# The order of work in the first block of an RWKV and Hadamard-FFN layer, and its last output rows in two banks

## The chip, the cores and the metric

The kernel runs on one core of a Trainium2 chip. Its engines are TensorE (PE, the matmuls), VectorE (DVE), ScalarE (ACT), GpSimd (POOL) and SyncE (SP), which here only issues DMAs. [...] The metric is the device time of one execution in microseconds; the number that counts is the median of several runs.

## What is computed

The input `x` has 4 sequences of 2048 tokens with 512 channels, in fp32. The layer is

```python
xn  = layernorm(x)                          # over the channels, no scale or shift
s   = xn shifted by one token               # zero before the first token of a sequence
r   = (mu_r*xn + (1-mu_r)*s) @ Wr.T         # the same for k and v
wkv = wkv_v4(k, v, w, u)                    # a recurrence over the tokens
att = (sigmoid(r) * wkv) @ Wo.T
h   = silu(xn @ W1.T) * (xn @ W3.T)         # 2048 hidden features
ffn = fwht(h) @ W2.T                        # Walsh-Hadamard transform over the 2048
out = x + att + ffn
```

## The kernel before

**Blocks.** The 8192 tokens are worked on in 8 blocks of `TB` = 1024 tokens. Tokens lie along the free dimension, channels on the 128 partitions: `xnT` holds a block of normalized activations as `NB` = 4 channel blocks of 128. A block has a projection stage (r, k, v), an up stage of 16 groups (one for each 128 features of W1 and W3), and a down stage of seven products (W2 with the Hadamard transform folded in, and Wo). From the second block on the projections, and in all blocks up and down, a 2x2 block product is made with seven products in place of eight, so that weights are brought into seven "forms". The recurrence (`wkv`) is cut into pieces that are handed out to DVE and ACT during the up stage by `step()`.

**Order.** All five engines are wrapped in `InOrder` (lines 24 to 36), which keeps each instruction in program order on its engine. So the order of the source is the order of each queue, and every row of the profile shows line 34, that of the wrapper. Groups of instructions are told apart by the names of their tiles: `bank` is PSUM, `tf` holds the mixed input of k (later, forms of the tokens), `hid` the hidden features, `part` the weight forms of an up group, `df` scratch for down forms, `dw` the down weights.

**PSUM.** There are eight banks of 128x512, given out in rotation by `bank()` (lines 89 to 91). A matmul into a bank waits until its last content has been read.

**The first block** (lines 553 to 615) can't be prepared during a block before it. The tokens come in two halves of 512 (`half`), and for each half:

- `first_statistics` (159): mean and variance of each token on DVE, and the power -0.5 on POOL.
- `first_spread` (162): per 128 tokens, a diagonal of the scale (made by DVE) and one of the shift (made by ACT), and two matmuls with a matrix of ones that spread scale and shift over all partitions into two banks.
- `first_normalized` (173): for each of four channel blocks, DVE multiplies and adds from these banks, and then `mixed_block` (180) mixes the block with its shifted self for k: ACT writes `(1-mu)*before` to `tf`, DVE adds `mu*here`.
- `projected` (196): four matmuls, one for each channel block, into one bank, and a copy by ACT to `k_sb`, `v_sb` or (with tanh) `r_sb`. There are four such groups for each half.

In between PE folds the Hadamard matrix into W2: `fold_products(n, m)` (419) multiplies rows n to m of `fold` (an alias of the upper half of `hid`), two matmuls for each row, and ACT evicts each at once with a scale. The eight rows are folded in four portions: rows 0 and 1 ahead of the first spread, 2 and 3 after it, 4 and 5 after the normalization of the second half, 6 and 7 in the second projection (v). The butterflies over these rows (`fold_butterflies`, 427) then run on DVE, and the third projection (r) follows.

**The up stage of the first block** (643 to 650) also makes the down weights. For group j below `NR` = 10, `down_forms(j)` (447) makes the forms on POOL from folded rows, or, for the last two, from Wo, which it loads first into a `df` tile; it stores them to `down_w`. Then `load_parts` for group j+2 loads a `part` and POOL makes its four forms. Both tile kinds come from rings: `ring_a` has three slots, `ring_b` two. SP issues all of these DMAs in this order, POOL makes all forms in this order.

**The down stage** (`down`, 475): seven products, each for two groups of 128 output rows, each of 10 matmuls of 512 columns. The last product's results are added to the residual by DVE (`c21`, 546) and stored by SP.

Of the kernel before, what the change touches and what calls it, by code (L numbers as in the profile page):

```python
# [8 lines left out]
F32 = mybir.dt.float32  # L9
AF = mybir.ActivationFunctionType  # L10
ALU = mybir.AluOpType
# [3 lines left out]
P = 128  # L15
H = 512
TB = 2 * H
TP = TB // P
OFF = 4
# [20 lines left out]
def tile_rwkv_attn_hadamard_ffn(  # L40
# [15 lines left out]
    NT, C = x.shape  # L56
    F = 2 * w2.shape[1] * P
    NB = C // P
    KH = NB // 2
    NF = F // P  # L60
    NR = (NF + NB) // 2
# [7 lines left out]
    ring_b = ctx.enter_context(tc.tile_pool(name="ring_b", bufs=2))  # L69
# [19 lines left out]
    def bank():  # L89
        turn[0] += 1  # L90
        return banks[(turn[0] - 1) % 8]
# [67 lines left out]
    def first_statistics(half):  # L159
        return token_statistics(f"f{half}", x_tok[:, half * HT : (half + 1) * HT, :])  # L160

    def first_spread(half, rs):
        diag = v_sb[:, half, :].rearrange("p (s t q) -> p s t q", s=2, q=P)
        for t in range(HT):
            dve.tensor_scalar(diag[:, 0, t], eye_sb, rs[:, 0, t : t + 1], None, ALU.mult)
            act.activation(diag[:, 1, t], eye_sb, AF.Copy, scale=rs[:, 1, t : t + 1])
        pts = []
        for s in range(2):
            pts.append(bank())
            pe.matmul(pts[s], lhsT=ones, rhs=diag[:, s].rearrange("p t q -> p (t q)"), start=True, stop=True)  # L170
        return pts

    def first_normalized(half, pts):
        for b in range(NB):
            xb = xnT[:, b, OFF + half * H : OFF + (half + 1) * H]
            dve.tensor_tensor(xb, xb, pts[0], ALU.mult)
            dve.tensor_tensor(xb, xb, pts[1], ALU.add)
            mixed_block(1, b, half * H, H)

    def mixed_block(kind, b, t0=0, n=TB):  # L180
        m = mix_of[kind][:, b, t0 : t0 + n]
        here, before = (xnT[:, b, OFF - d + t0 : OFF - d + t0 + n] for d in (0, 1))
        act.activation(m, before, AF.Copy, scale=omm[:, kind, b : b + 1])
        dve.scalar_tensor_tensor(m, here, vec[:, kind, b : b + 1], m, ALU.mult, ALU.add)

    def mixed(kind):
        for b in range(NB):
# [229 lines left out]
            sp.dma_start(out=fold[a].rearrange("p (k c) -> p k c", c=C), in_=w2[:, a])  # L417

    def fold_products(n, m):
        for a in range(n, m):  # L420
            for k in range(2):
                part = fold[a][:, ts(k, C)]
                pt = bank()
                pe.matmul(pt, lhsT=had_sb, rhs=part, start=True, stop=True)
                act.mul(part, pt, 0.5 / float(F) ** 0.5)

    def fold_butterflies():

# [15 lines left out]
            at[a], spare = spare, at[a]  # L444
        return sorted(enumerate(at), key=lambda p: p[1] is not e1)

    def down_forms(j, at):
        n, a = at[j] if j < NP else (j, None)
        t = ring_b.tile([P, 7, KH, P], F32, tag="b", name=f"df_{n}")
        far = down_w[:, :, n].rearrange("f p k c -> p f k c")  # L450
        if n < NP:
            a = a.rearrange("p (k m g c) -> p k m g c", k=2, m=2, c=P)
            seven_forms([t[:, f] for f in range(4)], a[:, 0, 0], a[:, 1, 0], a[:, 1, 1], a[:, 0, 1])
            sp.dma_start(out=far[:, 0], in_=a[:, 0, 0])
            sp.dma_start(out=far[:, 1:3], in_=a[:, 1])
            sp.dma_start(out=far[:, 3:7], in_=t[:, 0:4])
        else:
            sp.dma_start(out=t[:, 0:4], in_=wo[n - NP])
            forms_in(t)
            sp.dma_start(out=far, in_=t)  # L460

# [10 lines left out]

    order = (0, 1, 4, 6, 5, 3, 2)

    def down(i, w, between, w_after):
        y11, y12, y21, y22 = rows(0, 0), rows(0, 1), rows(1, 0), rows(1, 1)
        def product(k, pts, right, start, then):
            if k == 6:
                w_after()
            elif k:  # L480
                w.append(load_down(i, order[k + 1]))
            if k:
                next(between)
            for g in range(KH):
                for n in range(NR):
                    pe.matmul(
                        pts[g], lhsT=w[k][:, n, g, :], rhs=right[n // 2][:, n % 2, :],
                        start=start and n == 0, stop=n == NR - 1, skip_group_check=True,
                    )
                then(g)  # L490

        def difference(out, x0, x1):
            for o, p0, p1 in zip(out, x0, x1):
                dve.tensor_tensor(o, p0, p1, ALU.subtract)

        def at(mh, g, half):
            return ts(mh * KH + g, P), ds(i * TB + half * H, H)

        def residual(slot, mh, g, half):
            c, t = at(mh, g, half)  # L500
            sp.dma_start(out=slot, in_=xT[c, t])

        def store(slot, mh, g, half):
            c, t = at(mh, g, half)
            sp.dma_start(out=outT[c, t], in_=slot)

        add = dve.tensor_tensor
        pa, pb, pc = ([bank() for _ in range(KH)] for _ in range(3))
        s5 = [small.tile([P, H], F32, tag="s5", name=f"s5_{i}_d{g}") for g in range(KH)]
        for g in range(KH):  # L510
            residual(stage[g], 0, g, 0)
        product(0, pa, y11, True, lambda g: act.copy(pb[g], pa[g]))
        difference(y11, y12, y11)

        def c11(g):
            add(stage[g], pa[g], stage[g], ALU.add)
            store(stage[g], 0, g, 0)
            residual(stage[2 + g], 0, g, 1)
            residual(x22_of[g], 1, g, 1)

        product(1, pa, y21, False, c11)
        product(2, pc, y11, True, lambda g: act.copy(s5[g], pc[g]))
        difference(y12, y22, y12)
        for g in range(KH):
            add(x22_of[g], x22_of[g], s5[g], ALU.add)
        product(3, pc, y22, False, lambda g: None)
        difference(y22, y22, y11)

        def u2(g):
            act.copy(u2_of[g], pb[g])  # L530

        product(4, pb, y22, False, u2)
        difference(y21, y21, y22)
        for g in range(KH):
            add(u2_of[g], u2_of[g], stage[2 + g], ALU.add)
            add(stage[2 + g], pc[g], u2_of[g], ALU.add)
            store(stage[2 + g], 0, g, 1)
            residual(stage[g], 1, g, 0)

        def c22(g):  # L540
            add(x22_of[g], pb[g], x22_of[g], ALU.add)
            store(x22_of[g], 1, g, 1)

        product(5, pb, y12, False, c22)

        def c21(g):
            add(stage[g], pb[g], stage[g], ALU.add)
            store(stage[g], 1, g, 0)

        product(6, pb, y21, False, c21)  # L550


# [12 lines left out]
    load_channels(0, H, H)  # L565
    fold_load(4, NP)
    act.activation(weff, vec[:, 3, :], AF.Exp)
    fold_products(0, 2)
    spread_0 = first_spread(0, first_statistics(0))
    dve.tensor_scalar(omm, vec[:, 0:3, :], -1.0, 1.0, ALU.mult, ALU.add)  # L570
    dve.tensor_scalar(weff, weff, -1.0, None, ALU.mult)
    token_before(0)
    fold_products(2, 4)
    first_normalized(0, spread_0)
    first_rs = first_statistics(1)

    pending = {}
    for i in range(n_blocks):
# [13 lines left out]
        if i == 0:  # L592
            for kind, after in ((1, 2), (2, 0), (0, None)):
                w = w_next
                if after is not None:
                    w_next = load_square(i, after)
                    if kind != 1:
                        mixed(after)
                if kind == 2:
                    token_forms()  # L600
                for n in range(2 * NB):
                    if kind == 1:
                        if n == NB - 1:
                            spread_1 = first_spread(1, first_rs)
                        if n == NB:
                            first_normalized(1, spread_1)
                            fold_products(4, 6)
                            mixed(2)
                        projected(kind, w, n % NB, n // NB)
                    else:  # L610
                        projected(kind, w, n // 2, n % 2)
                    if kind == 2 and n == 2:
                        fold_products(6, NP)
                        folded = fold_butterflies()
            parts = [load_parts(i, 3 * KH + n) for n in range(2)]
        else:
# [25 lines left out]
        w_down = []  # L642
        for j in range(NF):
            if i == 0 and j < NR:
                down_forms(j, folded)
            if j + 2 < NF:
                parts.append(load_parts(i, 3 * KH + j + 2))
            if j >= NF - 2:
                w_down.append(load_down(i, order[j - NF + 2]))
            tail = up(i, j, parts.pop(0), tail, step)  # L650
# [29 lines left out]

        if not last:
            load_tokens(i + 1)
        down(i, w_down, (None for _ in range(6)) if last else next_tokens(), next_parts)


# [51 lines left out]
```

## Time and profile before

| | |
|---|---|
| timed runs, us | 3138.24, 3138.80, 3147.55; median 3138.8 |
| profiled execution, us | 3151.47 |
| its span, us | 3149.7 |
| PE busy | 3120.0 us, 99% |
| DVE busy | 2197.9 us, 70% |
| ACT busy | 874.1 us, 28% |
| POOL busy | 330.4 us, 10% |
| DMA | 334.44 MB, mean 106 GB/s |
| granted PE clock over the span | 0.995 |

The span is that of the profile, from its first to its last event; the execution's own time is 1.8 us longer. Times inside the span are counted from its start. By stage of the profiled execution:

| from to, us | what | PE busy, us | granted clock |
|---|---|---|---|
| 0 to 8.84 | loads, first statistics | 0 | 1.00 |
| 8.84 to 23.80 | folds, first spread | 11.89 | 1.00 |
| 43.16 to 60.39 | second spread, normalization | 12.12 | 0.96 |
| 74.26 to 132.62 | projections v and r | 58.36 | 1.00 |
| 132.62 to 241.94 | first block, up groups 0 to 8 | 108.32 | 1.00 |
| 241.94 to 273.57 | up groups 9 and 10 | 27.05 | 0.89 |
| 273.57 to 333.79 | up groups 11 to 15 | 60.22 | 1.00 |
| 333.79 to 3150 | first down stage, blocks 1 to 7 | 2812.06 | 1.00 |

A row of PE busy time is a sum over instructions whose ends are modelled; a fp32 matmul of the program is two MATMUL instructions. PE busy says that PE had work, not that it ran at its full clock.

### The profile page before, as it was taken

What the parts mean: (1) busy time and instruction counts of PE and PEld (TensorE: products, weight loads), DVE (VectorE), ACT (ScalarE), POOL (GpSimd) and SP (SyncE); (2) the same over time, 40 slices, a digit from 0 to 9 for tenths busy, and PEclk for the clock granted to TensorE, in tenths of its full rate; (3) what the DMA queues carried; (4) which work ended last, traced back from release to release, by engine and by line L of the source; (5) the groups of instructions that cost most, each with busy time, mean ns of one, the idle gap of its engine ahead of it and who ended that gap; (6) DMA issues with size and microseconds to landing.
All of it is one profiled execution on the core that took longest, in us unless ns stands there. A gap on an engine that the chain in (4) does not pass through costs nothing.

```text
span 3149.7 us, 20228 instructions
## 1 busy us (share of the span) xinstructions
PE 3120.0 (99%) x7232; PEld 1377.4 (44%) x7232; DVE 2197.9 (70%) x2316; ACT 874.1 (28%) x1374; POOL 330.4 (10%) x203
## 2 busy tenths in 40 slices
PE   7999999999999999999999999999999999999999
PEld 2443444444444444444444444444444444444444
DVE  4888856886478864787647876579655886658852
ACT  3232213331233302333023320333213332133310
POOL 1454112001000011000110001100011000110000
PEclk8999999999999999999999999999999999999999
DMA  4246433233322332222332224222332223322222
GB/s 149 79 150 228 144 110 107 82 125 110 117 72 82 114 127 102 82 72 112 134 107 82 71 102 159 93 72 80 132 123 99 71 82 146 123 75 80 76 100 77
DMA packets 75668, 334.44 MB, mean 106 GB/s; under 512 B 9136, under 2 KB 18352, under 8 KB 66224
## 3 DMA queue, kind: packets, MB, share of 16 engines
q1 hardware_dynamic: 75568, 333.15, 30.2%
q8 instruction: 57, 0.93, 0.1%
q14 instruction: 43, 0.35, 0.0%
HBM read 286.93 MB, written 46.19 MB: 106 GB/s over the span
## 4 chain that ended last, share of the span: by engine, by line
PE 98%; DMA 1%; DVE 1%; ACT 0%; issue 0%; SPq 0%; ACTq 0%
PE bank L34 98%; DMA part<-wpart 0%; DVE xnT L34 0%; DVE tf L34 0%; ACT tf L34 0%; DMA hid<-w 0%; ACT v_sb L34 0%; SPq L34 0%; DVE sa L34 0%; DVE bank L34 0%; DVE v_sb L34 0%; ACT k_sb L34 0%; ACT hid L34 0%; ACTq L34 0%
## 5 line engine op out<-in xcount | busy, mean ns | idle before, releaser
L34 PE MATMUL bank<-tf,part 128*128 128x512 f32 x2272 | 1043.0, 592 | 0.0
L34 PE MATMUL bank<-hid,dw 128*128 128x512 f32 x1792 | 787.3, 592 | 0.0
L34 PE MATMUL bank<-xnT,part 128*128 128x512 f32 x1536 | 723.8, 593 | 5.6 <-DMA part<-wpart 5.3
L34 PEld LDWEIGHTS bank<-tf,part 128*128 128x128 f32 x2272 | 432.0, 190 | 544.6 <-issue 515.7
L34 ACT COPY bank<-bank 128x512 f32<-128x512 f32 x526 | 299.8, 570 | 1258.7 <-PE bank L34 1257.5
L34 PEld LDWEIGHTS bank<-hid,dw 128*128 128x128 f32 x1792 | 340.5, 190 | 428.6 <-issue 426.7
L34 PEld LDWEIGHTS bank<-xnT,part 128*128 128x128 f32 x1536 | 292.1, 190 | 374.5 <-issue 364.5
L34 DVE SCALAR_TENSOR_TENSOR hid<-hid,bank 128x512 f32<-128x512 f32 x256 | 173.9, 679 | 175.0 <-ACT hid L34 174.8
L34 DVE TENSOR_TENSOR hid<-hid 128x1024 f32<-128x1024 f32 (+1 forms) x173 | 219.7, 1298 | 106.7 <-PE bank L34 105.8
L34 PE MATMUL bank<-hid,part 128*128 128x512 f32 x616 | 271.2, 592 | 0.0
L34 DVE RECIPROCAL e1b<-e1b 128x512 f32<-128x512 f32 x64 | 214.1, 3347 | 1.1
L34 PE MATMUL bank<-r_sb,dw 128*128 128x512 f32 x448 | 210.5, 592 | 0.0
L34 DVE TENSOR_TENSOR bank<-bank,s 128x512 f32<-128x512 f32 x256 | 168.2, 690 | 37.8 <-ACT bank L34 26.6
L34 ACT ACTIVATE hid<-bank 128x512 f32<-128x512 f32 x272 | 162.9, 600 | 101.9 <-PE bank L34 85.1
L34 DVE TENSOR_TENSOR hid<-hid,bank 128x512 f32<-128x512 f32 x256 | 173.5, 678 | 11.6 <-PE bank L34 7.1
L34 PEld LDWEIGHTS bank<-hid,part 128*128 128x128 f32 x616 | 117.0, 190 | 147.3 <-issue 145.4
L34 POOL TENSOR_TENSOR rs<-rs,neg_half 128x8 f32<-128x8 f32 x7 | 11.5, 1649 | 1581.6 <-DVE rs L34 1581.6
L34 DVE SCALAR_TENSOR_TENSOR hid<-xnT,vec,hid 128x1024 f32<-128x1024 f32 x64 | 93.0, 1487 | 99.9 <-ACT hid L34 99.9
L34 PEld LDWEIGHTS bank<-r_sb,dw 128*128 128x128 f32 x448 | 85.1, 190 | 107.1 <-issue 106.9
L34 ACT COPY s<-bank 128x512 f32<-128x512 f32 x128 | 75.0, 586 | 146.6 <-PE bank L34 146.6
L34 DVE TENSOR_TENSOR v_sb<-bank,v_sb 128x512 f32<-128x512 f32 x32 | 21.9, 688 | 130.2 <-PE bank L34 130.2
L34 POOL TENSOR_TENSOR tf<-xnT 128x1024 f32<-128x1024 f32 x16 | 46.5, 2904 | 599.3 <-PE bank L34 599.3
(103 smaller groups left out, 2238.9 us busy)
## 6 DMA issues: line engine op xcount, KB each, us to landing
part<-part_w SPq DMA_DIRECT2D x148, 896.0 KB, 4.6
dw<-down_w SPq DMA_DIRECT2D x56, 1280.0 KB, 6.4
part_w<-part SPq DMA_DIRECT2D x22, 896.0 KB, 6.9
k_sb<-x SPq DMA_DIRECT2D x7, 2048.0 KB, 8.3
xnT<-xT SPq DMA_DIRECT2D x7, 2048.0 KB, 9.4
v_sb<-xT SPq DMA_DIRECT2D x48, 256.0 KB, 4.4
out<-v_sb SPq DMA_DIRECT2D x48, 256.0 KB, 2.0
part<-wpart SPq DMA_DIRECT2D x22, 512.0 KB, 5.0
```

Of the source, the lines that this page charges most:

```text
L34: return self.tc.keep_in_program_order(issue(*args, **kwargs))
```

## The change

There are five edits.

1. `first_spread` is cut in two. `first_diagonals` makes the diagonals, and is called directly after the statistics; `first_spread` holds only the two matmuls. In the first half the second diagonal's four ACT instructions now come before any eviction of the fold.
2. `first_normalized` mixes one block behind the normalization: for block b DVE multiplies and adds, ACT writes the first term of block b (`mix_before`), and then DVE mixes block b-1 (`mix_here`). `mixed_block` calls both and is used as before elsewhere.
3. `fold_products` only issues matmuls and returns the list of what is to be evicted; `fold_evict` does that. The eight rows are folded as 0 ahead of the first spread, 1 and 2 behind it, 3 and 4 at the second half, 5 to 7 in the second projection. The evictions of the first two portions come behind the first half's normalization on ACT, those of the third behind the second half's.
4. `down_parts` allocates the `df` tile, and for the last two groups issues the load of Wo into it. It is called one group ahead of `down_forms`.
5. In the last block's down stage the last group of the last product is worked in two halves of 256 columns: the first in its own bank, the second in one more bank, to which ACT copies that half's partial sums. Each half is added and stored by itself. The extra bank is taken from the rotation in every block.

```diff
-    def first_spread(half, rs):
+    def first_diagonals(half, rs):
         diag = v_sb[:, half, :].rearrange("p (s t q) -> p s t q", s=2, q=P)
         for t in range(HT):
             dve.tensor_scalar(diag[:, 0, t], eye_sb, rs[:, 0, t : t + 1], None, ALU.mult)
             act.activation(diag[:, 1, t], eye_sb, AF.Copy, scale=rs[:, 1, t : t + 1])
+        return diag
+
+    def first_spread(diag):
         pts = []
...
     def first_normalized(half, pts):
-        for b in range(NB):
-            xb = xnT[:, b, OFF + half * H : OFF + (half + 1) * H]
-            dve.tensor_tensor(xb, xb, pts[0], ALU.mult)
-            dve.tensor_tensor(xb, xb, pts[1], ALU.add)
-            mixed_block(1, b, half * H, H)
...
+        for b in range(NB + 1):
+            if b < NB:
+                xb = xnT[:, b, OFF + half * H : OFF + (half + 1) * H]
+                dve.tensor_tensor(xb, xb, pts[0], ALU.mult)
+                dve.tensor_tensor(xb, xb, pts[1], ALU.add)
+                mix_before(1, b, half * H, H)
+            if b:
+                mix_here(1, b - 1, half * H, H)
+
+    def mix_before(kind, b, t0=0, n=TB):
+        m, before = mix_of[kind][:, b, t0 : t0 + n], xnT[:, b, OFF - 1 + t0 : OFF - 1 + t0 + n]
         act.activation(m, before, AF.Copy, scale=omm[:, kind, b : b + 1])
+
+    def mix_here(kind, b, t0=0, n=TB):
+        m, here = mix_of[kind][:, b, t0 : t0 + n], xnT[:, b, OFF + t0 : OFF + t0 + n]
         dve.scalar_tensor_tensor(m, here, vec[:, kind, b : b + 1], m, ALU.mult, ALU.add)
...
     def fold_products(n, m):
-        for a in range(n, m):
-            for k in range(2):
-                part = fold[a][:, ts(k, C)]
-                pt = bank()
-                pe.matmul(pt, lhsT=had_sb, rhs=part, start=True, stop=True)
-                act.mul(part, pt, 0.5 / float(F) ** 0.5)
+
+        left = []
+        for part in (fold[a][:, ts(k, C)] for a in range(n, m) for k in range(2)):
+            pt = bank()
+            pe.matmul(pt, lhsT=had_sb, rhs=part, start=True, stop=True)
+            left.append((part, pt))
+        return left
+
+    def fold_evict(left):
+        for part, pt in left:
+            act.mul(part, pt, 0.5 / float(F) ** 0.5)
...
-    def down_forms(j, at):
+    def down_parts(n):
+        t = ring_b.tile([P, 7, KH, P], F32, tag="b", name=f"df_{n}")
+        if n >= NP:
+            sp.dma_start(out=t[:, 0:4], in_=wo[n - NP])
+        return t
+
+    def down_forms(j, at, t):
         n, a = at[j] if j < NP else (j, None)
-        t = ring_b.tile([P, 7, KH, P], F32, tag="b", name=f"df_{n}")
...
-            sp.dma_start(out=t[:, 0:4], in_=wo[n - NP])
...
             for g in range(KH):
-                for n in range(NR):
-                    pe.matmul(
-                        pts[g], lhsT=w[k][:, n, g, :], rhs=right[n // 2][:, n % 2, :],
-                        start=start and n == 0, stop=n == NR - 1, skip_group_check=True,
-                    )
-                then(g)
+                whole = slice(0, H)
+                for pt, cols in ending if last and k == 6 and g == KH - 1 else [(pts[g], whole)]:
+                    for n in range(NR):
+                        pe.matmul(
+                            pt[:, cols], lhsT=w[k][:, n, g, :], rhs=right[n // 2][:, n % 2, cols],
+                            start=start and n == 0, stop=n == NR - 1, skip_group_check=True,
+                        )
+                    then(g) if cols == whole else c21(g, pt, cols)
...
+        ending = [(pb[KH - 1], slice(0, H // 2)), (bank(), slice(H // 2, H))]
...
+            if last and g == KH - 1:
+                act.copy(ending[1][0][:, H // 2 :], pb[g][:, H // 2 :])
...
-        def c21(g):
-            add(stage[g], pb[g], stage[g], ALU.add)
-            store(stage[g], 1, g, 0)
+        def c21(g, pt=None, cols=slice(0, H)):
+            add(stage[g][:, cols], (pb[g] if pt is None else pt)[:, cols], stage[g][:, cols], ALU.add)
+            c, t = at(1, g, 0)
+            sp.dma_start(out=outT[c, t][:, cols], in_=stage[g][:, cols])
...
-    fold_products(0, 2)
-    spread_0 = first_spread(0, first_statistics(0))
+    diag_0 = first_diagonals(0, first_statistics(0))
     dve.tensor_scalar(omm, vec[:, 0:3, :], -1.0, 1.0, ALU.mult, ALU.add)
     dve.tensor_scalar(weff, weff, -1.0, None, ALU.mult)
     token_before(0)
-    fold_products(2, 4)
+    left = fold_products(0, 1)
+    spread_0 = first_spread(diag_0)
+    left += fold_products(1, 3)
     first_normalized(0, spread_0)
-    first_rs = first_statistics(1)
+    fold_evict(left)
+    diag_1 = first_diagonals(1, first_statistics(1))
...
                         if n == NB - 1:
-                            spread_1 = first_spread(1, first_rs)
+                            spread_1 = first_spread(diag_1)
                         if n == NB:
+                            left = fold_products(3, 5)
                             first_normalized(1, spread_1)
-                            fold_products(4, 6)
+                            fold_evict(left)
                             mixed(2)
...
                     if kind == 2 and n == 2:
-                        fold_products(6, NP)
+                        fold_evict(fold_products(5, NP))
                         folded = fold_butterflies()
...
             if i == 0 and j < NR:
-                down_forms(j, folded)
+                t = down_parts(0) if j == 0 else t_next
+                t_next = down_parts(j + 1) if j + 1 < NR else None
+                down_forms(j, folded, t)
```

More of the change, by code (lines that the diff above doesn't have):

```diff
@@ L173, in first_normalized, with mixed_block @@
     def first_normalized(half, pts):
-        for b in range(NB):
-            xb = xnT[:, b, OFF + half * H : OFF + (half + 1) * H]
-            dve.tensor_tensor(xb, xb, pts[0], ALU.mult)
-            dve.tensor_tensor(xb, xb, pts[1], ALU.add)
-            mixed_block(1, b, half * H, H)
-    def mixed_block(kind, b, t0=0, n=TB):
-        m = mix_of[kind][:, b, t0 : t0 + n]
-        here, before = (xnT[:, b, OFF - d + t0 : OFF - d + t0 + n] for d in (0, 1))
+        for b in range(NB + 1):
[8 more added lines that the diff above has]
+        m, before = mix_of[kind][:, b, t0 : t0 + n], xnT[:, b, OFF - 1 + t0 : OFF - 1 + t0 + n]
         act.activation(m, before, AF.Copy, scale=omm[:, kind, b : b + 1])
+    def mix_here(kind, b, t0=0, n=TB):
+        m, here = mix_of[kind][:, b, t0 : t0 + n], xnT[:, b, OFF + t0 : OFF + t0 + n]
         dve.scalar_tensor_tensor(m, here, vec[:, kind, b : b + 1], m, ALU.mult, ALU.add)
+    def mixed_block(kind, b):
+        mix_before(kind, b)
+        mix_here(kind, b)
     def mixed(kind):
@@ L473, in tile_rwkv_attn_hadamard_ffn, with down @@
     order = (0, 1, 4, 6, 5, 3, 2)
-    def down(i, w, between, w_after):
+    def down(i, w, between, w_after, last):
         y11, y12, y21, y22 = rows(0, 0), rows(0, 1), rows(1, 0), rows(1, 1)
@@ L682, in tile_rwkv_attn_hadamard_ffn @@
             load_tokens(i + 1)
-        down(i, w_down, (None for _ in range(6)) if last else next_tokens(), next_parts)
+        down(i, w_down, (None for _ in range(6)) if last else next_tokens(), next_parts, last)
 def kernel(**inputs):
```

## The prediction

> **What bounds the kernel now.** I read the page's list of groups first, then the matmul engine's timeline over the first 70 us, then the chain of waits in order of time, then the busy time by windows. All program lines show as L34, the line of the ordering helper, so groups are told apart by tile names.
>
> The chain of waits (start, length, what) says where TensorE (PE) is not the bound:
>
> ```profile
> 22.24 0.72 ACT tf L34
> 22.99 0.75 DVE tf L34
> 23.74 0.61 DVE xnT L34
> 24.35 0.02 issue
> 24.37 0.70 DVE xnT L34
> 25.07 0.02 issue
> 25.09 0.73 ACT tf L34
> ...
> 60.39 175.48 PE bank L34 x403
> 235.87 5.93 DMA part<-wpart
> ...
> 252.28 6.11 DMA part<-wpart
> ...
> 273.57 2872.30 PE bank L34 x6692
> ```
>
> From 273.57 on, 6692 matmul rows take 2872.30 us, or 0.4292 us a row, with no wait. One matmul of the program (fp32, 512 columns) is two rows. The whole program has 7232 rows: at 0.4292 they need 3104.0 us. The first starts at 8.84 and the last ends at 3145.85 (3143.97 + 1.88), so 3145.85 - 8.84 - 3104.0 = 33.0 us are lost. Of these 24.2 lie before 74.26, the first matmul of the second projection (96 rows, 41.2 us of work, in 65.4 us), and 8.9 in the first block's up stage (132.62 to 333.79: 201.2 us for 448 rows, 192.3). Nothing else is to be had but the tail of 3.9 us behind the last matmul.
>
> PE's timeline shows the first half of the start (start, length, engine, operation, rows; idle time in brackets):
>
> ```profile
> 15.14 1.02 PE L34 MATMUL bank<-v_sb,ones 128*128 128x512 f32 x2
> 17.15 1.12 PE L34 MATMUL bank<-v_sb,ones 128*128 128x512 f32 x2 [0.99 <-ACT v_sb L34]
> 23.80 1.21 PE L34 MATMUL bank<-tf,w 128*128 128x512 f32 x2 [2.08 <-DVE tf L34]
> 26.65 2.07 PE L34 MATMUL bank<-tf,w 128*128 128x512 f32 x2 [1.65 <-DVE tf L34]
> 32.37 10.95 PE L34 MATMUL bank<-tf,w 128*128 128x512 f32 x18 [0.78 <-DVE tf L34]
> ```
>
> Each normalized block costs 2.86 us (23.80 to 26.65), because VectorE (DVE) waits for ScalarE's (ACT's) first mixing term and only then goes to the next block. And PE, starved, runs slow: 18 rows take 10.79 us from 32.37 to 43.16, where 7.73 would do. The granted clock (third figure from the end of a line of the windows view) says the same:
>
> ```profile
> 23.80:43.16 19.36, 16.14 (x24) 5.90 (x25) 9.85 (x25) 3.34 (x5) 1.01 (x1) 0.65 0.32 128
> 60.39:74.26 13.87, 13.87 (x27) 5.99 (x27) 4.87 (x4) 6.90 (x10) 2.33 (x1) 0.81 0.01 1
> ```
>
> The second half repeats the pattern, and its last block comes at 60.39.
>
> **The start, first half.** The first eight rows run cold: 8.84 to 15.14, so 0.857 us a row for most. Before, they are the fold of rows 0 and 1; after, four fold rows and the four spread rows. ACT's diagonals no longer stand behind four evictions (they began at 15.84): the statistics end at 9.58, four of 0.39 us end near 10.9, before PE asks at 12.3. So the first spread ends at 8.84 + 6 x 0.857 = 14.0 and the second at 15.14. DVE starts 0.2 later, as it did (16.0 to 16.20): multiply at 14.2, first add at 15.35 instead of 18.32. The channels are there: issue at 4.14, landing 8.5 us later, 12.6. DVE then runs without ACT in its loop, 0.61 + 0.70 + 0.75 = 2.06 a block: first add done 16.05, three blocks to 22.2, the last mix to 22.95, against 32.32 before.
>
> PE cannot use all of it. The banks go round by eight: two for the fold, two for the spread, four for the next fold, so the first projection gets bank 0, which is not evicted until ACT is through its four mixing terms (the last add ends 21.45, ACT's term 22.2, eviction 22.85). PE's fold ends at 18.6 (8 rows after 15.14), and it idles 4.3 us to 22.9. **Here a rule speaks against the change.** The row: the idle of 4.34 us ahead of 258.53 was followed by 12 rows in 7.76 us (258.53 to 266.29), 2.6 over the 5.15 they need; the stretch at 32.37 lost 3.06. The Trainium skill ("TensorE: Matmul & The Clock Gate", Part 1) puts the clock at half after an idle window of about 3.4 us, and back after 3.4 us of work, in a free-running window; by that the loss would be half of 3.4, 1.7 us, and a hole of 4.3 need not always hold a whole idle window. The trace is harsher: at 26.65 it is slow after two holes of 2.08 and 1.65 with work between. I take 2.8, bounds 0 and 3.1.
>
> So the projection's first three groups, 24 rows, run from 22.9 for 10.3 + 2.8 to 36.0; before, this point was 43.16. The second statistics (5.0 us on DVE) start at 22.95 and are hidden, as are ACT's second diagonals, done by 29.
>
> **The start, second half.** Spread 36.0 to 37.7, fourth group to 41.15, and two more folds, 8 rows, to 44.6. ACT's queue decides: the first mixing term stands behind the copy of the fourth group, as it does now (copy 3.64 us after the group's start, term 0.48 later). Copy at 41.35, term 41.83 to 42.55, first mix 42.6 to 43.35, then two blocks of 2.06: 45.4 and 47.45, last mix 48.3. PE takes the first block at 44.6, the second at 45.45, waits 1.2 for the third, and has the last at 48.36. The row at 241.94 (idle 1.00, then 4 rows in 1.95) says that such a hole does not slow it, so the 2.7 lost after 60.39 (26 rows in 13.87, 11.16 needed) goes too. The remaining 26 rows end at 59.5, against 74.26: 14.8 less. One fold (4 rows, 1.7 us) is moved behind this point, into the gap after the third group of the second projection. **Sum of the start: -13.0 us.** If ACT or DVE takes 10% longer in those loops, about 2 us go; without the cold stretch it is -15.8.
>
> Behind this PE is dense to the up stage, so the gain is kept. The moved fold adds two evictions ahead of the butterflies; DVE needs that part 5 us into the first pass, and is behind its own mixing until then. Cost 0; uncovered, 1.7.
>
> **Wo's parts.** The stall of the up stage is a loop: SyncE's queue (SP) issues the next part only behind the store of the down forms; GpSimd (POOL) makes these only after the forms of the part before.
>
> ```profile
> 238.26 0.42 SPq L34 DMA_DIRECT2D df<-wo  x1
> 241.93 5.03 POOL L34 TENSOR_TENSOR part<-part 128x256 f32<-128x256 f32 x4 [6.56 <-PE bank L34]
> 246.91 4.87 POOL L34 TENSOR_TENSOR df<-df 128x256 f32<-128x256 f32 x4
> 251.81 0.37 SPq L34 DMA_DIRECT2D down_w<-df  x1
> ```
>
> Wo was issued at 238.26 and landed about 7.3 later, 245.6; POOL reaches it at 246.91 with no idle, busy with the part. Loading it a group earlier moves nothing on this path. The load now sits on SP ahead of the seventh group's stores and waits there for the slot of the sixth (stored 218.65, landing 3.3 later, 222): behind it are stores and the form store of 235.4, 13 us later, so no cost. What may be won is traffic: the part issued at 252.28 no longer shares with Wo at 254.08, 6.1 against the median 5.3 us. I take -0.2, bounds -0.8 and +0.5; the stall itself stays.
>
> **The last rows.** The last group's 20 rows become 40 of 256 columns. No row of the trace has 256 columns. If the weight load (0.19 us busy) stays beside a row of 0.215, it costs nothing; if each of the 20 added loads stood bare, 3.8 us. The skill's page of TensorE ("Back-to-back issue gap") gives 262 cycles for 256 columns and 518 for 512, which over two passes and 40 rows is an estimate of 0.1 us; I take that, because 0.19 is under 0.215. DVE's last add shrinks from 0.69 to about 0.42 (by 512 columns and the 0.28 of a 128-column operation), and the store is halved: stores of 256 and 128 KB landed in 2.1 and 1.7. Sum 0.1 - 0.27 - 0.4 = -0.6, bounds -0.7 and +3.1. ACT's half copy lies in an idle ACT, over 4 us before its use. The extra bank per block turns the rotation by one in seven transitions: the fifth bank of the next stage is then the last one of the down stage, read by DVE at 454.16 to 454.85 and wanted 20 rows, 8.6 us, after 453.96. Slack 7.7; cost 0.
>
> **Sum** against the profiled run (3151.47 us, span 3149.7): -13.0 - 0.2 - 0.6 = -13.8. The timed runs are 3138.24, 3138.80 and 3147.55: the last lies 8.75 above the median, about the 8.9 of the up stage's stalls, so I read the median as a run without them and leave the Wo term out: 3138.8 - 13.6 = **3125.2**.
>
> **Rivals.** (1) Likeliest, 0.66: as above, 3121 to 3129; the no-cold case, 3122.4, is in it. (2) The start is cheaper without the profiler: profiled minus median is 12.7, the stalls explain 8.9, the other 3.8 may be start that timed runs don't lose. Then the gain is 13.6 - 3.8 = 9.8: 3129.0. For it: the median's loss over the floor is only some 20; against: the waits are sums of instruction times. 0.16. (3) The up stage stalls in the median run: 3125.2 + 8.9 = 3134.1. For it: the loop's part issues at 203.04, 219.14, 235.87 are 16 us apart where PE needs 12.0; against: one timed run of three. 0.14. (4) Slower: that loop falls behind sooner. Each further group late costs 4.3 (16.3 - 12.0) and a cold 2.6; two such groups cancel the gain, and over three more make 3138.8 - 13.6 + 8.9 + 3 x 6.9 = 3154.8. It decides if the butterflies end later relative to the up stage than now. Against: they start behind mixing that moves with the second projection (-14.8), so 1.7 earlier relative to it. 0.04. That the Wo change doesn't do what it says is part of all four.
>
> About 0.3%, 9.4 us, is what a measurement can tell from no change: faster is below 3129.4. Case 1 is wholly there, case 2 in two of three, case 3 is within: faster 0.77, same 0.19, slower 0.04. The range 3119.5 to 3134.5 takes in the missing cold stretch and case 3.
>
> **What would show it.** Right: the first spread ahead of the second fold; a hole near 4 us ahead of the first projection with DVE long ahead; second projection at 59 to 60; block 0's up stage still short of a part near the ninth and tenth group; DVE's last add near 0.42. Wrong: a hole ahead of each projection block as now, a wait behind 273 in a later block, or rows over 0.22 us in the last group.

## The result and the profile after

| | before | after |
|---|---|---|
| timed runs, us | 18: 3137.37 to 3153.59, median 3138.9 | 18: 3124.75 to 3137.65, median 3127.69 |
| profiled execution, us | 3151.47 | 3126.89 |
| its span, us | 3149.7 | 3125.1 |
| first matmul | 8.84 | 8.86 |
| second projection begins | 74.26 | 57.34 |
| PE waits for a part in the up stage | 1.00 and 4.34 | none |
| last matmul's end to the end of the span | 3.85 | 3.3 |

The medians differ by 11.2 us, where 13.6 were forecast (3125.2 us, range 3119.5 to 3134.5). The ratio of the times is 0.9958, 95% interval [0.9946, 0.9971], which is 9 to 17 us less. The two profiled executions lie further apart, 24.6 us, because that of the kernel before had a stall in the up stage and slow rows in the start that most of its timed runs lack.

PE's timeline of the changed kernel over the start (start, length, engine, operation, rows, idle time and releaser):

```profile
8.86 3.75 PE L34 MATMUL bank<-hid,had_sb 128*128 128x512 f32 x4 [8.86 <-DMA hid<-w]
12.41 2.02 PE L34 MATMUL bank<-v_sb,ones 128*128 128x512 f32 x4
14.27 3.60 PE L34 MATMUL bank<-hid,had_sb 128*128 128x512 f32 x8
21.73 12.26 PE L34 MATMUL bank<-tf,w 128*128 128x512 f32 x24 [3.87 <-ACT hid L34]
...
45.20 12.30 PE L34 MATMUL bank<-tf,w 128*128 128x512 f32 x28 [0.86 <-DVE tf L34]
57.34 10.46 PE L34 MATMUL bank<-hid,w 128*128 128x512 f32 x24
```

The last row ahead of the second projection in the kernel before was this one:

```profile
60.39 14.03 PE L34 MATMUL bank<-tf,w 128*128 128x512 f32 x26 [1.73 <-DVE tf L34]
```

Between the first matmul and the second projection nine waits have become two. The first is the one for bank 0: 3.87 us, released by ACT's eviction to `hid`. The second is for the third block of the second half, 0.86 us. The chain of waits shows DVE without ACT in its loop, and PE dense from 45.20 to the end:

```profile
17.14 0.61 DVE xnT L34
17.75 0.02 issue
17.77 0.69 DVE xnT L34
18.46 0.66 DVE tf L34
19.12 0.61 DVE xnT L34
...
45.20 3076.61 PE bank L34 x7188
```

A block is 0.61 + 0.02 + 0.69 + 0.66 = 1.98 us (17.14 to 19.12), where it was 2.86. The windows view has PE at a granted clock of 0.92 (third figure from the end) from 23.80 to 40.00, where it was 0.65 from 23.80 to 43.16, and at 1.00 in the next stretch:

```profile
23.80:40.00 16.20, 16.20 (x36) 7.06 (x35) 4.65 (x17) 4.05 (x10) 1.01 (x1) 0.92 0.38 153
40.00:60.00 20.00, 19.14 (x46) 8.04 (x45) 11.07 (x13) 12.55 (x18) 4.92 (x3) 1.00 0.07 17
```

### The profile page after: what moved, and what is told of

It reads as the page before. It is cut to its first block, busy times and chain, and to the rows that moved or that the text cites. A ratio compares the mean times of both kernels' runs of the same rounds, so it can differ in the third digit from the quotient of the medians.

```text
span 3125.1 us, 20283 instructions
## 1 busy us (share of the span) xinstructions
PE 3108.2 (99%) x7252; PEld 1378.9 (44%) x7252; DVE 2197.2 (70%) x2317; ACT 873.9 (28%) x1375; POOL 322.6 (10%) x203
## 4 chain that ended last, share of the span: by engine, by line
PE 99%; DVE 0%; DMA 0%; SPq 0%; issue 0%; ACT 0%; ACTq 0%
PE bank L34 99%; DVE xnT L34 0%; DMA hid<-w 0%; DVE tf L34 0%; SPq L34 0%; ACT tf L34 0%; ACT hid L34 0%; DVE v_sb L34 0%; ACTq L34 0%; ACT k_sb L34 0%
## 5 line engine op out<-in xcount | busy, mean ns | idle before, releaser
L34 PE MATMUL bank<-hid,dw 128*128 128x512 f32 (+1 forms) x1808 | 787.5, 588 | 0.0
L34 PE MATMUL bank<-r_sb,dw 128*128 128x512 f32 (+1 forms) x452 | 210.7, 588 | 0.0
L34 DVE TENSOR_TENSOR hid<-hid,bank 128x512 f32<-128x512 f32 x256 | 173.6, 678 | 11.5 <-PE bank L34 7.1
L34 POOL TENSOR_TENSOR rs<-rs,neg_half 128x8 f32<-128x8 f32 x7 | 11.5, 1648 | 1581.1 <-DVE rs L34 1581.1
L34 DVE TENSOR_TENSOR v_sb<-bank,v_sb 128x512 f32<-128x512 f32 (+1 forms) x33 | 22.1, 672 | 129.9 <-PE bank L34 129.9
```

The lines of the kernel that those rows point to most:

```text
L34: return self.tc.keep_in_program_order(issue(*args, **kwargs))
```

## The experiments

All times are medians of the timed runs. The kernel before ran beside each set; its runs come in groups near 3138, 3142, 3147 and 3152 us, so groups are compared with like groups where that matters. The lower group is the one near 3138.

**The start alone.** The changed kernel with the edits to Wo's load and to the last rows taken back.

```diff
-                t = down_parts(0) if j == 0 else t_next
-                t_next = down_parts(j + 1) if j + 1 < NR else None
-                down_forms(j, folded, t)
+                down_forms(j, folded)
...
-                for pt, cols in ending if last and k == 6 and g == KH - 1 else [(pts[g], whole)]:
```

> The first block's start as changed (diagonals first, one block ahead, folds and evictions moved), without the edits to Wo's load and to the last rows. My theory: the start is all but 0.6 us of the gain, so 3128.3 us median, 0.6 above the changed kernel, and as large a share of runs some 10 us higher as in both kernels. Rival: loading Wo a group earlier is what keeps the up stage fed; then this kernel loses part of the gain (3131 or more) and most of its runs show the stall of about 9 us.

Five runs, 3126.25 to 3128.91, median 3126.65; the lower group of the kernel before was at 3137.2 to 3138.5. None of the five was high. The start is nearly all of the gain. The time came out below the changed kernel's 3127.69, not 0.6 above: the two are from different sets, and 0.6 can't be read across them.

**Wo alone.** The kernel before with `down_parts` called one group ahead.

> The kernel before with Wo's parts loaded one group ahead and nothing else. My theory: GpSimd reaches Wo with no idle anyway, so no change, 3138.9 us within 0.5, and the runs 9 to 14 us above the median stay as frequent (5 of 18). Rival: the edit feeds the up stage; then the high runs go, the highest is below 3143 and the median falls by up to 1.

3138.67 us in 14 runs (3137.1 to 3147.21), ratio 0.9996 [0.9988, 1.0005]. No change of the time, as forecast. High runs don't vanish: one of 14 here and four of 18 in the changed kernel lie 9 us or more above the lowest group. With five, four, one and three of 18, 19, 20 and 17 in the kernel before, these counts are too small to tell a share apart.

**Mixing order alone.** The kernel before with the new `first_normalized`, `mix_before` and `mix_here`, the rest of the start as it was.

> The kernel before with only the normalization running one block ahead of the mixing; folds, evictions and diagonals as before. My theory, worked out as in the prediction: last mix of the first half 28.6 instead of 32.3, second projection at 64.1 instead of 74.3 of the profiled execution, so -10 against a run like that and -7 against the common run, 3131 us. Rival: the diagonals and the moved evictions carry the larger half, since ScalarE reaches the first mixing term only at 22.2; then less than 5 us come off, 3134 or more.

3128.67 us (five runs, 3128.35 to 3131.18), ratio 0.9963 [0.9949, 0.9977]. Against the lower group of the kernel before in this set (nine runs, median 3137.76) it is 9.1 us less, two more than forecast. PE's timeline of this kernel:

```profile
22.57 1.72 PE L34 MATMUL bank<-tf,w 128*128 128x512 f32 x2 [2.08 <-DVE tf L34]
24.55 10.86 PE L34 MATMUL bank<-tf,w 128*128 128x512 f32 x22 [0.26 <-DVE tf L34]
...
60.01 10.46 PE L34 MATMUL bank<-hid,w 128*128 128x512 f32 x24
```

The second projection begins 51.9 us behind the first matmul (8.13 to 60.01), in the changed kernel 48.5 (8.86 to 57.34). Of these 3.4 us 1.7 are the fold row that the changed kernel does only later; the other 1.7 are what all the rest of the reordered start gives. In the times it is 2.0, from here to the 3126.65 of the start alone in the same set. The 22 rows took 10.70 us (24.55 to 35.25, where the second spread begins), 1.3 more than at 0.4292 a row; the granted clock was at half from 23.0 to 26.4.

**Bank 0 evicted early.** The changed kernel, with fold row 0's two evictions ahead of the normalization.

```diff
+    fold_evict(left[:2])
     first_normalized(0, spread_0)
-    fold_evict(left)
+    fold_evict(left[2:])
```

> The changed kernel with the two evictions of fold row 0 put ahead of the first half's normalization, where ScalarE idles from 10.8 to 15.2; the other four stay behind it. My theory: the idle of 3.87 us ahead of the first projection is the wait for bank 0; without it three of its four matmuls lie beside the normalization and the next group starts 22.9 instead of about 25 to 26, so -2.4 us if the clock falls in the smaller holes, -4.1 if it stays up: 3123.6 to 3125.3. Rival: the normalization itself is the bound and the wait is an accident of order; then PE ends the first group no earlier and less than 1 us comes off.

3123.63 us in six runs: 3122.41, 3122.53, 3122.57, 3124.70, 3133.68 and 3134.30. The lower four have a median of 3122.55, some 1 us better than the range that was forecast. The profiled execution was the one of 3133.68, and shows both the gain and a stall:

```profile
18.00 2.31 PE L34 MATMUL bank<-tf,w 128*128 128x512 f32 x4
21.17 8.87 PE L34 MATMUL bank<-tf,w 128*128 128x512 f32 x20 [0.86 <-DVE tf L34]
29.88 1.88 PE L34 MATMUL bank<-v_sb,ones 128*128 128x512 f32 x4
...
235.61 1.95 PE L34 MATMUL bank<-xnT,part 128*128 128x512 f32 x4 [1.81 <-DMA part<-wpart]
253.34 3.75 PE L34 MATMUL bank<-xnT,part 128*128 128x512 f32 x4 [5.48 <-DMA part<-wpart]
```

The projection begins at 18.00, and the second spread 21.7 us behind the first matmul (8.15 to 29.88) instead of 25.0 (8.86 to 33.83): 3.2 us less, with 20 rows in 8.71 us and a granted clock of 1.00. So the wait for bank 0, with the slow rows behind it, was the cost of that order. The two waits at 235.61 and 253.34 are the stall of the profiled kernel before, in a kernel that has Wo loaded a group ahead.

**The hole filled.** The changed kernel, with the last fold matmul done four more times ahead of the normalization, into the same bank.

```diff
+    for _ in range(4):
+        pe.matmul(left[-1][1], lhsT=had_sb, rhs=left[-1][0], start=True, stop=True)
     first_normalized(0, spread_0)
```

> The changed kernel with the last fold matmul of the first half done four times more (the same result again) in the hole ahead of the first projection, 8 rows or 3.4 us of PE work in a hole of 3.9; nothing else waits for it. It parts the cold clock from the wait. My theory: the projection starts at the same place, and its 24 rows take 10.3 us instead of the 12.1 of the changed kernel, so -1.8 us, 3125.4 to 3125.9. Rival: the slow rows have another cause than the hole; then the 24 rows still take 12.1 and the time stays at 3127.3.

3125.05 us (six runs, 3124.32 to 3125.28), 0.35 below the range that was forecast. PE's timeline of this kernel, and a line of its windows view:

```profile
14.20 7.03 PE L34 MATMUL bank<-hid,had_sb 128*128 128x512 f32 x16
21.65 10.57 PE L34 MATMUL bank<-tf,w 128*128 128x512 f32 x24 [0.43 <-ACT hid L34]
32.06 1.88 PE L34 MATMUL bank<-v_sb,ones 128*128 128x512 f32 x4
```

```profile
23.80:40.00 16.20, 16.20 (x39) 7.22 (x38) 5.91 (x19) 4.97 (x11) 1.01 (x1) 1.00 0.36 144
```

The projection starts at nearly the same place, its 24 rows take 10.41 us (21.65 to 32.06) instead of 12.10 (21.73 to 33.83), and the granted clock is 1.00 instead of 0.92. So the half clock behind the hole costs 1.7 us; matmuls that compute nothing new win it back. The medians lie 2.6 apart, but they are from different sets.

**The last rows alone.** The kernel before with the two banks and nothing else.

> The kernel before with the last output rows in two banks and nothing else. My theory, by the changed kernel's trace (last add 0.42 instead of 0.69, 40 rows in 8.63 us against 8.58, end 3.3 us behind PE instead of 3.85): -0.5 us, so the common runs at 3137.3 where those of the kernel before lie at 3137.8. Rival: the extra bank turns the rotation in every block and costs at the seven transitions; then 1 us or more is added.

14 runs, 3136.87 to 3152.90, and the profiled one was of the lower group. That group has a median of 3137.39 (seven runs), against 3138.26 (13 runs) in the kernel before; the next has 3141.51 (five) against 3142.26 (six). That is 0.8 us less in each. The median over all, 3139.54, says nothing, as seven of 14 runs are in the higher groups. No cost of the turned rotation shows.

**The kernel before again.**

> The kernel before, once more under the profile. Its timed runs come in groups near 3138, 3142, 3147 and 3152, and the profiled one, 3151.5, was of the last. My theory: the first two groups differ by how many rows of the start run at half clock, so a run near 3138 shows one of the cold stretches (18 rows from about 32, 26 rows from about 60) shorter or gone, and no wait for a part. Rival: they differ by waits for DMAs at the start.

This run was a high one, 3151.35 us, with waits for a part of 3.09 and 2.65, so it did not show the lower group. The run with the last rows alone (3137.39) and that with Wo alone (3142.01) do, since their start is that of the kernel before. One line of each, the last block of the second half:

```profile
58.30 11.43 PE L34 MATMUL bank<-tf,w 128*128 128x512 f32 x26 [1.73 <-DVE tf L34]
```

```profile
59.81 14.06 PE L34 MATMUL bank<-tf,w 128*128 128x512 f32 x26 [1.73 <-DVE tf L34]
```

The first is from the lower group, the second from the next: the same 26 rows behind the same waits, 2.6 us apart. With the first eight rows (7.85 to 13.42 and 8.09 to 14.50, 0.8 apart) and the 18 rows of the first half (10.41 and 10.84) this is 3.9 of the 4.2 us between the groups. The granted clock over the 26 rows was 1.00 in the first and 0.81 in the second. So these two groups differ in the clock, not in a wait. Five profiled executions have this start, and all five agree: the 26 rows took 11.43 us in those of 3137.39 and 3138.70 us, and 14.02 to 14.06 in those of 3142.01, 3151.35 and 3151.47.

**The next part ahead of the down forms.** Bank 0 early, and in the up stage the part's load and forms moved ahead of the down forms on both SP and POOL.

```diff
-                down_forms(j, folded, t)
             if j + 2 < NF:
                 parts.append(load_parts(i, 3 * KH + j + 2))
+            if i == 0 and j < NR:
+                down_forms(j, folded, t)
```

> The changed kernel with bank 0 evicted early (as in the run before) and, in the first block's up stage, the next part's load and forms issued ahead of the down forms instead of behind them. My theory: the stall of 7 to 10 us in some runs comes from a loop in which the part's load waits on SyncE behind the store of down forms that GpSimd makes only after the part before; with the part first its load waits for its ring slot alone (one group of PE, 12.0 us), so no run stalls: all within 3121.5 to 3126, median 3122.6, and part issues about 12 us apart where they were 16. Rival: GpSimd's own work, 6 to 11 us a group beside a busy VectorE, is the bound; then a quarter of the runs still lie some 10 us higher.

3152.24 us (3149.99 to 3156.94), with five waits for a part of 19.2 us together: the theory missed here. SP's queue of this kernel:

```profile
170.43 0.37 SPq L34 DMA_DIRECT2D down_w<-df  x1
170.85 0.50 SPq L34 DMA_DIRECT2D part_w<-part  x1
175.63 0.34 SPq L34 DMA_DIRECT2D part<-wpart  x1
```

The load at 175.63 goes into the slot of a part whose store stood behind the down forms' store, and was issued only at 170.85. So the store's 4.8 us stand in series with the load, the forms and the down forms; parts are issued 15 to 20 us apart.

**Only the stores behind.** As the run before, but POOL's order is kept, and SP issues the stores of the down forms behind the load of the next part.

```diff
-            sp.dma_start(out=far[:, 0], in_=a[:, 0, 0])
-            sp.dma_start(out=far[:, 1:3], in_=a[:, 1])
-            sp.dma_start(out=far[:, 3:7], in_=t[:, 0:4])
+            return [(far[:, 0], a[:, 0, 0]), (far[:, 1:3], a[:, 1]), (far[:, 3:7], t[:, 0:4])]
...
+                stores = down_forms(j, folded, t)
             if j + 2 < NF:
                 parts.append(load_parts(i, 3 * KH + j + 2))
+            for out, in_ in stores:
+                sp.dma_start(out=out, in_=in_)
```

> The changed kernel with bank 0 evicted early and, in the first block's up stage, only the stores of the down forms moved on SyncE behind the load of the next part; GpSimd's order stays. My theory after the run with the part ahead on both queues (which put two DMAs, the store of a part and the load of the next into its slot, in series behind the down forms): a part's load may not stand on SyncE behind work that waits for GpSimd. Here it waits for its slot alone, whose part was stored a group earlier, so parts are issued 12 us apart, no run stalls, all within 3121.5 to 3126, median 3122.6. Rival: GpSimd's own 6 to 11 us a group and the landing make the loop; then issues are 14 us or more apart and a quarter of the runs lie 9 us or more higher.

3123.13 us (five runs, 3122.41 to 3123.24), ratio to the kernel before 0.9944 [0.9932, 0.9957], and SP issues a part every 12.02 us:

```profile
173.13 0.35 SPq L34 DMA_DIRECT2D part<-wpart  x1
185.14 0.34 SPq L34 DMA_DIRECT2D part<-wpart  x1
197.16 0.33 SPq L34 DMA_DIRECT2D part<-wpart  x1
```

The same edit of the stores on the kernel before:

> The kernel before with the same edit of the stores and nothing else. My theory: its groups of runs near 3147 and 3152 (6 of the 39 of the last two rounds) go, those near 3138 and 3142 stay, since these differ by cold rows in the start: median 3138 to 3142, none above 3144. Rival: the high groups are no stall of the up stage; then they stay.

13 runs, 3138.17 to 3143.46, none higher; the kernel before beside it had three of 17 at 3146 to 3147. The time of a run without a stall did not fall: the median is 3139.49, the ratio 0.9998 [0.9990, 1.0006], and by like groups these runs lie 1.0 to 1.6 us above those of the kernel before (3139.17 against 3137.55, and 3142.92 against 3141.93). The cause of that is open.

Here the issues around Wo slip: parts are issued at 224.99, 238.40 and 252.54, which is 13.4 and 14.1 us apart instead of 12.02. In this kernel Wo's load stands on SP directly ahead of the part; in the run above, where it is a group ahead, nothing slips. That fits a use of the Wo edit once the stores are out of the way, but the two kernels differ in their start as well, and no run parts the two.

## Why the prediction was right

It was right in direction and mechanism. The sum came nearer than its parts did: the start gave about 2.2 us more than forecast, and the base from which it was taken off was some 3.7 us too high. That the two errors partly cancel is luck.

| step | forecast | measured |
|---|---|---|
| first multiply, first add | 14.2, 15.35 | 13.61, 14.47 |
| last mix of the first half ends | 22.95 | 21.98 |
| PE idle for bank 0 | 4.3 | 3.87 |
| first projection begins | 22.9 | 21.73 |
| its 24 rows | 13.1 | 12.10 |
| second spread | 36.0 | 33.83 |
| wait for the third block | 1.2 | 0.86 |
| second projection begins | 59.5 | 57.34 |
| last add; end behind PE | 0.42; 3.3 | 0.42; 3.3 |

**The start, waits.** Each wait that was to go went, and each that was to come came, at its place and with its releaser. The times lie about 1 us early because the first eight rows took 5.4 us (8.86 to 14.27) and not 6.3, and because a block on DVE takes 1.98, not 2.06. The 0.9 us on the eight rows is luck too: over the profiled executions they took 5.6 to 6.4 us with the start of before and 5.1 to 6.1 with the changed one.

**The start, clock.** Of the two sizes for the cold stretch behind the hole, the rule of the Trainium skill ("TensorE: Matmul & The Clock Gate", Part 1: half clock until about 3.4 us of work) was nearer than the row I took: 1.7 against 2.8, and 1.8 by the trace (12.10 less 10.30), 1.7 by the filled hole. Read in windows of 0.1 us, the granted clock of the changed kernel is at half from 22.93 to 26.35, 3.4 us, and falls only 1.2 us after the hole has ended. The row I took it from, 7.76 us for 12 rows, came behind a hole of 4.34, and such stretches vary: behind the same waits, the same 26 rows in the unchanged start took 11.43 or 14.06. The page calls the window free-running, and the number of cold matmuls run-variable. The traces agree: in the kernel before the clock is at half from 24.71 to 38.36 and from 58.84 to 65.67, which is four and two times 3.41 us, with starts that lie ten times 3.41 apart.

They do not bear out an idle window of 3.4 us. When the clock fell at 24.71, PE had behind it one hole of 2.08 us and 0.9 us of work, and not yet the hole of 1.65 that the prediction counts with it.

**The base.** This is the term that was most off in size: I laid a sum made against one profiled execution on the median. The profiled execution of before had the 26 rows at half clock and the stall; the common one has neither. Against an execution like it (24.2 us lost before the second projection) the start gave 24.2 - 9.0 = 15.2, more than the 13.0 forecast. Against the lower group (20.5 lost, from the run with the last rows alone: 69.56 - 7.85 - 41.2) it gave 11.5. That run and the changed kernel's share the edit of the last rows and lie 10.5 us apart (3137.39 and 3126.89); the first matmul came 1.0 later in the second (8.86, not 7.85), so the sum closes. The second rival said that 3.8 us of the start might not be lost in timed runs and forecast 3129.0. Its reason held, and the experiments gave it its cause: rows at half clock, 3.9 us. The time came between it and the likeliest case since the changed kernel's own start was 2.2 us better than forecast (57.34, not 59.5).

**Wo's parts.** That the edit alone moves nothing held (3138.67 us, ratio 0.9996), and the reason with it. POOL's timeline of the changed kernel reaches Wo with no idle, 20 us after its load was issued at 200.06:

```profile
215.80 4.05 POOL L34 TENSOR_TENSOR part<-part 128x256 f32<-128x256 f32 x4 [5.81 <-PE bank L34]
219.80 3.02 POOL L34 TENSOR_TENSOR df<-df 128x256 f32<-128x256 f32 x4
```

**The stall.** "The stall itself stays" held: the run with bank 0 early shows it in its profile. Four of the 18 timed runs of the changed kernel are near 3137, as far above the rest as a stall would put them, but none of them was profiled. That the median would be without it held too. The third rival, the stall in the median, did not come, nor did the fourth; but the loop that both rest on is real. With the stores out of it no run of 18, in two kernels, was in a stalled group. In the kernel before 13 of 74 runs were, so by chance alone none of 18 would come about 3 times in 100 (an estimate from that share).

**The last rows.** This is the first of the four rows of the profile for the last group, in the changed kernel:

```profile
3113.00 3.62 PE L34 MATMUL bank<-hid,dw 128*128 128x256 f32 x16
```

The 40 rows took 8.63 us (3113.00 to the end near 3121.6), and 20 of 512 columns would take 8.58: no weight load stands bare. The end behind PE fell by 0.55 in the trace and 0.8 by like groups of timed runs, forecast 0.6. The turned rotation costs nothing in the changed kernel: PE is dense from 45.20 on.

**A better version.** Bank 0 evicted early and the stores behind the next part's load give 3123.13, 4.6 us below the changed kernel's median, which is from another set. The five runs lie within 0.9 us. Next to the lower runs with bank 0 early alone (3122.55) the stores make no run faster; what they take away, as far as 18 runs tell, is the stall.

## What to carry to other kernels

When a loop crosses engines block by block, take the crossing out first: running DVE one block ahead of what ACT returns gave 9 us by itself, and the reordering around it 2, with 3 to 4 more once the bank that the new order tied up was freed. When evictions are put off, follow the bank rotation to the next user of each bank; here two of six evictions had to stay early. On an in-order DMA queue, a load that the critical engine needs soon must not stand behind a store that waits for another engine, nor behind the store that frees its own slot; and before a sum is laid on a median, look at which of its cold rows and stalls the profiled execution had.

## What the runs showed of the hardware

- The granted clock of PE was 1.00 or half, and half for 3.4, 6.8 or 13.6 us at a time in the first 85 us of every profiled execution that has such a stretch. In all six executions with a hole of 2.08 us ahead of the first projection it fell within 1.1 us of the end of that hole.
- Behind the same waits such a stretch comes and goes between executions: behind two holes of 1.73 us, with 1.1 us of work between, 26 rows took 11.43 us in two executions and 14.02 to 14.06 in three. This makes groups of times 4.2 us apart.
- The first eight rows took 5.1 to 6.4 us where 3.4 would do at 0.4292 a row. The granted clock reads 1.00 there, so that they ran at half clock is inferred from their length alone (0.857 us a row at first).
- A hole of 0.86 us did not slow PE (20 rows in 8.71 with bank 0 early; 28 rows in 12.14, from 45.20 to 57.34, in the changed kernel).
- POOL's forms of 128x256 took 0.73 us at best and up to 2.70. That one ran from 198.18 to 200.88 in the kernel before, beside a scan of 128x1024 on DVE (198.00 to 200.35). A busy DVE is not enough: four forms took 3.02 us from 219.80 in the changed kernel, where DVE was busy for 2.98 of them. A group of eight took 6 to 13 us.
- Matmul rows of 256 columns cost half of those of 512, weight load included (8.63 us for 40).
